# One extra matmul per step, into unused rows of the sums' PSUM tile

## The chip, the cores and the metric

The kernel runs on one core of a Trainium2 chip. The core has five engines that run at the same time, each through its own list of instructions in order: PE (TensorE, matrix multiplies; its weight loads are listed apart as PEld), ACT (ScalarE), DVE (VectorE), POOL (GpSimd) and SP (SyncE, which here only issues DMA transfers). An instruction that needs another engine's result waits for a semaphore, and everything behind it on its own engine waits too. The metric is the device time of one execution in microseconds (us); lower is better.

## The reference, cut to what matters

Four layers run one after the other on a tensor of shape 8 x 56 x 56 x 192. Layer 0 has a convolution branch and a branch with a selective scan; layers 1 and 2 are selective scans alone; layer 3 is windowed attention followed by an MLP. The part around which everything is arranged is the scan. For each image, each of three scan layers, and each of four directions k over the 56 x 56 positions:

```
def step(h, t):
    u_t, d_t, b_t, c_t = t
    h = jnp.exp(d_t[..., None] * A) * h + (d_t * u_t)[..., None] * b_t[:, :, None, :]
    return (h, jnp.einsum('bkdn,bkn->bkd', h, c_t))
scan_in = (jnp.moveaxis(xs4, -1, 0), jnp.moveaxis(delta, -1, 0), jnp.moveaxis(Bs, -1, 0), jnp.moveaxis(Cs, -1, 0))
h0 = jnp.zeros((B, K, D_INNER, D_STATE), x.dtype)
_, ys = lax.scan(step, h0, scan_in)
ys = jnp.moveaxis(ys, 0, -1) + Ds[None, :, :, None] * xs4
...
yv = _ln(yv, out_norm_g, out_norm_b) * jax.nn.silu(z)
```

There are 192 channels (d) with 16 states (n) each, so 3072 independent recurrences over 3136 positions, for 8 x 3 x 4 combinations of image, layer and direction. The sum over n with the weights c gives y, the four directions are added up, and a layer norm follows.

## The kernel before, in words

**Units and steps.** A unit (`Unit`) is one image, layer, direction and one quarter of the positions (784 of 3136); there are 8 x 3 x 4 x 4 = 384 of them. A unit is worked off in 24 steps: 2 halves of the channels (`h`, 96 each), 4 groups of 4 states (`sg`), 3 groups of 32 channels (`j`). One step holds 32 channels x 4 states = 128 recurrences on the 128 partitions. The loop in `run` goes over 9216 steps, and 8 more to drain, and writes the instruction lists of all engines in that order.

**What a step does.** `make` has ACT compute x = exp(A * delta) into one of two PSUM tiles (`ps_x`) and POOL compute db = (delta * u) * B. One step later DVE runs the recurrence as a scan (`ps_x<-ps_x,state,db` in the profile, or `hc<-ps_x,...` in every fourth step) and multiplies by C into `hc` (in every fourth step POOL multiplies instead). Two steps later ACT copies the last column to `state`, for the unit that continues there, 24 steps on. `hc` has 8 buffers.

**The sums.** Every third step, `add_up` has PE add three `hc` tiles into the PSUM tile `ps_y`: six matmuls (three channel groups j, two halves q of the columns) with the 0/1 matrix `esum` (128 x 32) as weights, `ps_y<-hc,esum` in the profile. The results of j = 0, 1, 2 go to partitions 0-31, 32-63 and 64-95. Partitions 96-127 of the two banks hold nothing. There is one such tile (`psum1`, bufs=1). After four `add_up` (12 steps) a sum is complete, and two steps later `merge` has ACT copy it to the layer's output (`act<-ps_y`). The next `add_up` starts a new tile, with two full matmuls that bring in D * u or the sum of the earlier directions (`ps_y<-act,dd`, `ps_y<-act,ident`).

**Background pieces.** All other work (the first layer's convolutions and projections of the next image, layer norms, the projection of delta, B and C, the attention and the MLP of the image before) is written as Python generators that yield between pieces. At the end of each step, `run` lets them issue pieces while a budget per engine lasts (`SPARE`, `MOST`; costs in `Engines` and `Meter`). A piece that multiplies on PE takes one of two PSUM banks (`ps_p`), and its result is fetched by ACT or DVE at the earliest one step later (`LAG = 1`). So in each engine's list, the pieces of a step follow the scan work of the step. `ahead` is the queue of pieces that prepare the next half unit (delta through softplus, du, and the transfers that spread them), `urgent` that of the layer norms and projections, `back` the rest.

**Order.** `in_order` ties each engine's instructions to the order in which they were written. A trailing part, after the last step, runs the attention of the last image alone, with more PSUM banks (`ps_t`).

Nearly all instructions carry the line of the helper that counts their cost (L109), so they are told apart by their tiles. A matmul on fp32 operands is two MATMUL records in the profile, with a weight load each.

Of the kernel before, what the change touches and what calls it, by code (L numbers as in the profile page):

```python
# [38 lines left out]
C = 192  # L39
CH = 96  # L40
# [8 lines left out]
HC = CK // 2  # L49
# [89 lines left out]
class Net:  # L139
# [146 lines left out]
    def l3_constants(self):  # L286
# [5 lines left out]
        with self.tc.tile_pool(name="setup", bufs=1) as sp:  # L292
# [12 lines left out]
            for name in ("pb", "f2b"):  # L305
# [3 lines left out]
                nc.tensor.matmul(p, self.ones, v, start=True, stop=True)  # L309
                yield LAG  # L310
                nc.vector.reduce_sum(mean[:CH, :1], p, axis=AX.X)
# [12 lines left out]
            for m in range(4):  # L324
                held = yield from self.bank()
                p = held[:, :NT]
                nc.tensor.matmul(p, w1[:, 128 * m : 128 * m + 128], tab, start=True, stop=True)
                yield LAG
                nc.scalar.activation(hid[:, m, :], p, AF.Identity, bias=b1[:, m : m + 1])
# [6 lines left out]
            for m in range(4):  # L336
                nc.tensor.matmul(p, w2[:, m, :], hid[:, m, :], start=m == 0, stop=m == 3)
            yield LAG

# [88 lines left out]
    def ln_cm(self, x, n, sq):  # L428
# [4 lines left out]
        for c in range(2):  # L433
            nc.tensor.matmul(p, self.ones, x[:, c, :], start=c == 0, stop=c == 1)
        yield LAG
        for c in range(2):
# [5 lines left out]
    def to_norm(self, x, n, sq):  # L442
# [6 lines left out]
        for c in range(2):  # L449
            nc.tensor.matmul(p, self.ones, sq[:, c, :], start=c == 0, stop=c == 1)  # L450
        yield LAG
        nc.scalar.activation(p, p, AF.Ln, bias=self.eps[:CH], scale=1.0 / C)
# [47 lines left out]
    def ssm_front(self, b):  # L500
# [3 lines left out]
        with tc.tile_pool(name="f1", bufs=1) as f1, tc.tile_pool(name="f2", bufs=2) as f2:  # L504
# [30 lines left out]
            def gate(xnt, r, e, sz):  # L535
                held = yield from self.bank()
                p = held[:CH, :T]
                nc.tensor.matmul(p, win[:, CH * e : CH * e + CH], xnt, start=True, stop=True)
                yield LAG
                if e < 2:  # L540
# [275 lines left out]
    def run(self):  # L816
        nc = self.nc
        self.B = self.a["x"].shape[0]
        units = []
        for g in range(3 * self.B):  # L820
            for o, k in enumerate((0, 1, 3, 2) if g % 2 == 0 else (2, 1, 3, 0)):
                for n, i in enumerate(range(NC) if k < 2 else range(NC - 1, -1, -1)):
                    units.append(Unit(g, k, i, n, o))
        for n, U in enumerate(units[1:]):
            units[n].next = U
        self.ranked, self.ending = None, False
        self.use_ln_exp()
        self.new_image(0)
        self.back.append(Task(self.ssm_front(0)))
        self.back.append(Task(self.conv_front(0)))  # L830
        for i in range(NC):
            self.urgent.append(Task(self.after(-1, i)))
        self.urgent.append(Task(self.columns(0)))
        self.state = self.s1.tile([128, NG], F32, name="state")
        self.B_, self.C_, self.spread = {}, {}, {}

        steps = [
            (U, h, sg, j) for U in units for h in range(2) for sg in range(NSG) for j in range(3)
        ]
        S = len(steps)  # L840
        half = NG // 2
        self.step = 0
        self.ahead.append(Task(self.prepare(units[0], 0, 0)))
        self.need(("half", 0))
        self.ahead.append(Task(self.prepare(units[0], 1, half)))
        for sg in range(NSG):
            self.load_bc(units[0], sg)
        made, weighed, copies = {}, {}, deque()
        left = dict.fromkeys(self.load, 0.0)
        for s in range(S + 8):  # L850
            self.now += 1
            self.step = s
            for e in left:
                left[e] = min(left[e] + SPARE[e], MOST[e])

            t = s + half + 1
            if t < S and t % half == 0:
                self.ahead.append(Task(self.prepare(*steps[t][:2], t)))
            if s < S and s % half == 0:
                self.need(("half", s))  # L860
                U = steps[s][0]
                if s % (16 * NG) == 0:
                    if U.l == 0:
                        self.begin_image(U.b)
                    self.dd = self.s1.tile([CH, 2, CH], F32, name="dd")
                    for c in range(2):
                        nc.scalar.activation(
                            self.dd[:, c, :], self.ident[:CH, :CH], AF.Copy,
                            scale=self.dsum[:, U.l, c : c + 1],
                        )  # L870

            t = s - 2
            if 0 <= t < S and not steps[t][0].last:
                U, h, sg, j = steps[t]
                end = CK - 1 if U.k < 2 else 0
                nc.scalar.copy(self.at_state(h, sg, j), made[t][:, end : end + 1])
            made.pop(t, None)
            if s < S:
                made[s] = self.make(*steps[s])
            t = s - 1  # L880
            if 0 <= t < S:
                U, h, sg, j = steps[t]
                x, db = made[t]
                pool = t % 4 == 3
                hc = self.s6.tile([128, CK], F32, name="hc")
                hs = hc if pool else x
                sense = slice(None) if U.k < 2 else slice(None, None, -1)
                nc.vector.tensor_tensor_scan(
                    hs[:, sense], x[:, sense], db[:, sense],
                    0.0 if U.first else self.at_state(h, sg, j), ALU.mult, ALU.add,  # L890
                )
                if not pool:
                    nc.vector.tensor_mul(hc, hs, self.C_[U, sg])
                made[t] = hs
                weighed[t] = hc
            t = s - 2
            if 0 <= t < S and t % 4 == 3:
                U, h, sg, j = steps[t]
                nc.gpsimd.tensor_mul(weighed[t], weighed[t], self.C_[U, sg])
            t = s - 4  # L900
            if 0 <= t < S and t % 3 == 2:
                U, h, sg, j = steps[t]
                self.add_up(U, h, sg, [weighed.pop(t - 2 + d) for d in range(3)])
                if sg == NSG - 1:
                    copies.append((s + 2, U, h))
            if copies and copies[0][0] <= s:
                self.merge(*copies.popleft()[1:])
            before = dict(self.load)
            while self.piece(self.ahead):
                pass  # L910
            self.spend(left, before)
            for queue in (self.urgent, self.back):
                while min(left["PE"], left["ACT"]) > 0.0 and self.piece(queue):
                    before = self.spend(left, before)

            t = s - 4
            if 0 <= t < S and t % NG >= half and t % 3 == 2:
                n = t // NG + 1
                if n < len(units):
                    self.load_bc(units[n], t % half // 3)  # L920
        while copies:
            self.merge(*copies.popleft()[1:])
        while any([self.piece(self.urgent, True), self.piece(self.back, True)]):
            self.now += 1

        self.ending = True
        self.scans.close()
        with self.tc.tile_pool(name="pst", bufs=1, space=bass.MemoryType.PSUM) as ps:
            self.banks += [ps.tile([128, 512], F32, name=f"ps_t{n}") for n in range(6)]
            self.back.append(Task(self.attention_block(self.B - 1, ENDS)))  # L930
            while self.piece(self.back, True):
                self.now += 1
        self.in_order()

    def spend(self, left, before):
        for e in left:
            left[e] -= self.load[e] - before[e]
        return dict(self.load)
# [116 lines left out]
    def add_up(self, U, h, sg, hcs):  # L1055

        nc = self.nc
        k, i = U.k, U.i
        u, y = self.bufs[U.g % 2], self.bufs[(U.g + 1) % 2]
        if sg == 0:  # L1060
            p = self.ps("y", CH, 1024).rearrange("p (q n) -> p q n", q=2)[:, :, :HC]
            for q in range(2):
                w, t = (self.dd[:, h, :], u) if U.begins else (self.ident[:CH, :CH], y)
                nc.tensor.matmul(
                    p[:, q, :], w, view(t, k, h, i * CK + q * HC, HC), start=True, stop=False
                )
            U.sums[h] = p
        p = U.sums[h]
        for q in range(2):
            for j, hc in enumerate(hcs):  # L1070
                nc.tensor.matmul(
                    p[G * j : G * j + G, q, :], self.esum, hc[:, q * HC : (q + 1) * HC],
                    start=False, stop=sg == NSG - 1,
                )
# [352 lines left out]


LAG = 1
HCS = 8  # L1430

ENDS = 5
# [130 lines left out]
```

## Time and profile before

| what | value |
|---|---|
| time, median of 3 runs | 26609.99 us (26607.5 to 26614.08) |
| the profiled execution's own time | 26624.15 us |
| its span, first to last instruction | 26622.0 us |
| mean granted TensorE clock | 0.76 of full speed |
| PE busy (matmuls) | 18403.8 us |
| DVE busy | 24146.0 us |
| POOL busy | 23082.9 us |
| ACT busy | 17059.2 us |
| 26622.0 us over 9216 steps | 2.89 us a step |

In the page of the profile, a group is one row: line, engine, operation, output<-inputs, count, then the busy time of the group, the mean of one in ns, and the idle time of the engine just before instructions of the group with what ended most of it. "PEclk" is the clock that PE was granted, in tenths. A row of the waits says who waited for whom, the sum in us, how often, and the longest. A row of the timeline is start, duration, engine, operation, tiles, shapes, how many in a row, and in brackets the idle time before it.

### The profile page before, as it was taken

The page shows a single profiled execution, that of the slowest core. Times are in us where ns is not written, and L with a number is a line of the kernel's source. Part 1 is how long each engine was busy: PE and PEld are TensorE (multiplying, and loading weights), DVE is VectorE, ACT ScalarE, POOL GpSimd, SP SyncE. Part 2 cuts the span into 40 slices and gives each one's busy share as a digit, 9 for nine tenths or more (in the row PEclk, how much of TensorE's full clock was granted, in tenths as well). Part 3 has the DMA queues.
Part 4 walks back from the last instruction along what each step waited for, and adds up shares of the span by engine and source line. Part 5 has one row for each costly group of instructions (what it writes and reads, how often), then busy time and mean ns, then how long its engine had stood idle before and what let it go on. Part 6 is the DMA issues. An engine that isn't in the chain of part 4 may idle for free. (4 is left out here: it accounts for less than half of the span.)

```text
span 26622.0 us, 260231 instructions
## 1 busy us (share of the span) xinstructions
PE 18403.8 (69%) x76788; PEld 6418.9 (24%) x76788; DVE 24146.0 (91%) x19164; ACT 17059.2 (64%) x30413; POOL 23082.9 (87%) x13255
## 2 busy tenths in 40 slices
PE   6675567776676767767767676677766777677657
PEld 2221122222222222222222222222222222222214
DVE  5999999999999999998999999999899999999994
ACT  4655566666666656666666766667666676666654
POOL 5888988988889888898888988988888888889992
PEclk7776777777777777777777777777777777777767
DMA  4565565556555566555655556555565555655551
GB/s 95 136 140 121 133 138 135 131 128 140 138 133 131 129 140 137 133 130 129 143 134 135 131 130 143 133 131 129 132 142 132 133 129 135 139 133 134 130 131 41
DMA packets 1503447, 3472.21 MB, mean 130 GB/s; under 512 B 310618, under 2 KB 503219, under 8 KB 1502020
## 3 DMA queue, kind: packets, MB, share of 16 engines
q1 hardware_dynamic: 1496452, 3455.15, 56.7%
q8 instruction: 606, 9.93, 0.1%
q0 software_dynamic: 3072, 0.31, 0.1%
q14 instruction: 821, 6.73, 0.1%
q10 hardware_dynamic: 2496, 0.09, 0.0%
HBM read 1457.23 MB, written 147.89 MB: 60 GB/s over the span
## 5 line engine op out<-in xcount | busy, mean ns | idle before, releaser
L109 POOL TENSOR_TENSOR db<-usp,bt 128x784 f32<-128x784 f32 x9216 | 16851.6, 1857 | 118.6 <-DMA usp<-du 71.4
L109 DVE TENSOR_TENSOR_SCAN ps_x<-ps_x,state,db 128x784 f32<-128x784 f32 x5184 | 9564.9, 1845 | 623.1 <-ACT state L109 266.7
L109 ACT ACTIVATE ps_x<-dsp,A 128x784 f32<-128x784 f32 x9216 | 8444.0, 917 | 2515.6 <-DVE hc L109 2290.5
L109 PE MATMUL ps_y<-hc,esum 128*32 128x392 f32 x36864 | 6882.9, 639 | 1045.1 <-POOL hc L109 696.0
L109 DVE TENSOR_TENSOR hc<-ps_x,ct 128x784 f32<-128x784 f32 x6912 | 6736.8, 975 | 654.1 <-DVE ps_x L109 11.5
L109 POOL TENSOR_TENSOR hc<-hc,ct 128x784 f32<-128x784 f32 x2304 | 4249.2, 1844 | 2448.1 <-ACT state L109 1901.2
L109 ACT COPY state<-ps_x 128x1 f32<-128x1 f32 x5184 | 823.5, 159 | 4579.7 <-DVE hc L109 4558.4
L109 DVE TENSOR_TENSOR_SCAN hc<-ps_x,state,db 128x784 f32<-128x784 f32 x1728 | 3180.1, 1840 | 230.5 <-ACT state L109 109.6
L109 DVE TENSOR_TENSOR_SCAN ps_x<-ps_x,db 128x784 f32<-128x784 f32 x1728 | 3084.8, 1785 | 275.8 <-ACT state L109 120.0
L109 PEld LDWEIGHTS ps_y<-hc,esum 128*32 128x32 f32 x36864 | 1601.2, 130 | 5928.8 <-issue 3126.8
L109 PE MATMUL ps_y<-act,ident 96*96 96x392 f32 x2304 | 1610.2, 835 | 1694.5 <-ACT act L109 1682.9
L109 PE MATMUL ps_p<-act,act 13*96 13x392 f32 (+1 forms) x3072 | 1502.9, 605 | 969.1 <-ACT s L109 294.9
L109 POOL TENSOR_TENSOR du<-delta,act 96x784 f32<-96x784 f32 x768 | 1566.5, 2040 | 66.4 <-ACT delta L109 63.9
L109 PE MATMUL ps_p<-act,wx 96*88 96x392 f32 (+1 forms) x1536 | 985.4, 778 | 627.0 <-ACT delta L109 313.4
L109 ACT ACT_TABLE_LOAD x896 | 1149.6, 1283 | 29.5 <-PE ps_p L109 13.6
L390 ACT ACT_TABLE_LOAD x897 | 1150.9, 1283 | 15.9
L109 DVE TENSOR_TENSOR_SCAN hc<-ps_x,db 128x784 f32<-128x784 f32 x576 | 1024.7, 1779 | 68.5 <-ACT state L109 35.6
L109 PEld LDWEIGHTS ps_y<-act,ident 96*96 96x96 f32 x2304 | 469.8, 226 | 2520.1 <-ACT act L109 1984.1
L109 PE MATMUL ps_p<-xip,diag 96*96 96x448 f32 x2016 | 864.0, 580 | 104.3 <-ACT delta L109 103.6
L109 ACT COPY act<-ps_y 96x784 f32<-96x784 f32 x768 | 928.0, 1208 | 8.5 <-PE ps_y L109 8.5
L109 PEld LDWEIGHTS ps_p<-act,act 13*96 13x96 f32 (+1 forms) x3072 | 471.1, 180 | 1887.5 <-issue 377.5
L109 ACT COPY state<-hc 128x1 f32<-128x1 f32 x1728 | 325.2, 188 | 866.6 <-DVE hc L109 863.9
(222 smaller groups left out, 18022.9 us busy)
## 6 DMA issues: line engine op xcount, KB each, us to landing
dsp<-delta SPq DMA_DIRECT2D x2304, 392.0 KB
usp<-du SPq DMA_DIRECT2D x2304, 392.0 KB
bt<-bcd SPq DMA_DIRECT2D x1536, 392.0 KB
ct<-bcd SPq DMA_DIRECT2D x1536, 392.0 KB
wf<-in_wf SPq DMA_DIRECT2D x128, 288.0 KB
wf<-wf2d SPq DMA_DIRECT2D x128, 288.0 KB
bcd<-bcx SPq DMA_DIRECT2D x256, 134.8 KB
szd<-sz SPq DMA_DIRECT2D x56, 336.0 KB
```

The source lines that it names most:

```text
L109: return call(out, *args, **k)
L390: self.tc.nc.scalar.preload_act_table_set(LN_EXP)
```

## The change

`add_up` now takes all 128 partitions of the `ps_y` tile and keeps rows 96-127 as `self.idle`. A new method `warm(n)` issues n matmuls into those rows: weights `esum[:96]` (96 x 32), moving operand `wout` (96 x 384), each with start and stop set, to the first bank for the first and the second bank for the second. It is called at three places of each step, with the counts in `WARM = (0, 0, 1)`: so once a step, behind the last background piece. It does nothing until the first `ps_y` tile exists. Nothing reads the result. `warm` calls TensorE directly, not through the meter, so the budget does not see it, and every other instruction of every engine stays in the same order. I call the new matmul the pad below.

```diff
@@ run
+        self.idle = None
         self.ranked, self.ending = None, False
...
             if copies and copies[0][0] <= s:
                 self.merge(*copies.popleft()[1:])
+            self.warm(WARM[0])
             before = dict(self.load)
             while self.piece(self.ahead):
                 pass
+            self.warm(WARM[1])
             self.spend(left, before)
             for queue in (self.urgent, self.back):
                 while min(left["PE"], left["ACT"]) > 0.0 and self.piece(queue):
                     before = self.spend(left, before)
+            self.warm(WARM[2])
...
+    def warm(self, n):
+
+        for q in range(n if self.idle is not None else 0):
+            self.tc.nc.tensor.matmul(
+                self.idle[:, q % 2, : 2 * C], self.esum[:CH], self.wout.rearrange("p m c -> p (m c)"),
+                start=True, stop=True,
+            )
...
@@ add_up
         if sg == 0:
-            p = self.ps("y", CH, 1024).rearrange("p (q n) -> p q n", q=2)[:, :, :HC]
+            p = self.ps("y", 128, 1024).rearrange("p (q n) -> p q n", q=2)[:, :, :HC]
+            self.idle, p = p[CH:], p[:CH]
...
 LAG = 1
+WARM = (0, 0, 1)
 HCS = 8
```

In the instruction lists of the two kernels, as built, PE has 9218 more matmuls (from the seventh pass of the loop to its last, 9224 - 6), and the other engines have the same work in the same order. Some waits differ. `merge`, which waited (where it waited for PE at all) for the last `add_up` of its sum, now waits in all 768 cases for a pad, that of the step before it. The first pad after a `merge` waits for ACT where before the first matmul of the next tile did (650 cases in both lists), and that first matmul now waits for PE's own pad.

## The prediction

> **What bounds the kernel now.** First the page: busy time by engine, and the slices with PE's granted clock.
>
> ```profile
> span 26622.0 us, 260231 instructions
> PE 18403.8 (69%) x76788; PEld 6418.9 (24%) x76788; DVE 24146.0 (91%) x19164; ACT 17059.2 (64%) x30413; POOL 23082.9 (87%) x13255
> ...
> PE   6675567776676767767767676677766777677657
> ...
> DVE  5999999999999999998999999999899999999994
> ...
> PEclk7776777777777777777777777777777777777767
> ```
>
> DVE is busy in nine tenths of nearly every slice: it sets the pace, 2.89 us a step. PE has 8218 us to spare and runs at 0.76 of its clock throughout. Then the waits, DVE's and ACT's:
>
> ```profile
> DVE ps_x L109 <- ACT state L109: 386.6, 315, 52.5
> DVE ps_x L109 <- ACT ps_x L109: 252.6, 182, 5.7
> ...
> DVE ps_p L109 <- PE ps_p L109: 65.2, 31, 39.0
> DVE act L109 <- PE ps_p L109: 60.2, 65, 6.6
> ```
> ```profile
> ACT state L109 <- DVE hc L109: 5422.3, 4498, 15.3
> ...
> ACT bcx L109 <- PE ps_p L109: 268.8, 135, 11.0
> ACT hid L109 <- PE ps_p L109: 145.6, 172, 3.5
> ACT xw L109 <- PE ps_p L109: 99.9, 38, 12.2
> ```
>
> DVE's 2476 us outside its busy time are partly short gaps between dependent instructions; counted over the trace, gaps above 150 ns make 1754 us. DVE hardly waits for PE itself, it waits for ACT when ACT is late, and ACT is late for one because it stood before a bank that PE had not filled. Counted over the 9216 steps, ACT waits 1020 us for PE, DVE 87 us. That is all that a better PE could give back. Third, the timeline of PE, where it had idled and where it had not:
>
> ```profile
> 13008.73 4.17 PE L109 MATMUL ps_p<-act,ones 96*96 96x392 f32 x6 [5.92 <-ACT act L109]
> 13012.74 1.48 PE L109 MATMUL ps_y<-act,ident 96*96 96x392 f32 x4
> 13014.15 1.52 PE L109 MATMUL ps_y<-hc,esum 128*32 128x392 f32 x12
> ```
> ```profile
> 13008.00:13012.00 4.00, 3.27 (x5) 1.52 (x6) 3.81 (x4) 1.76 (x3) 4.00 (x3) 0.50 0.12 49
> ...
> 13016.00:13020.00 4.00, 3.92 (x20) 1.38 (x18) 3.97 (x4) 2.07 (x5) 1.39 (x2) 1.00 0.51 77
> ```
>
> The second fence gives stretches with busy times by engine (PE first), then the clock, 0.50 and 1.00. After 5.92 us of idle PE runs at half clock (weight loads, and so matmul records, follow each other every 0.65 us), and some 4 us later at full clock (every 0.33 us).
>
> **What the change adds, step by step.** (1) Nothing is removed; 9218 pads are added on PE. A pad is two records of 96x384; by the nearest rows of 96x392 it costs 2 x 0.33 = 0.66 us at full clock, 1.30 us at half clock. The lower bound is nothing: twelve esum records took 1.52 us, four turns of 0.35 us and not twelve, so matmuls into different 32-row strips run beside each other, and a pad directly behind an `add_up` could too. Most pads follow a piece or another pad in the same strip, so I take 0.66 us: 6084 us of PE's 8218 us. Other engines get no instruction, SP and the DMA queues neither.
>
> (2) Where the pads run. A pad has no input of its own, so it doesn't wait until its step comes: PE runs it at once behind the matmul ahead of it in the list. In the 5.92 us of idle time above the two or three pads in front of the waiting matmul take 1.3 to 3.9 us, and the rest stays idle. So long gaps shrink but many remain. Counted over the trace, 832 gaps of PE exceed 3.4 us (5012 us together).
>
> The Trainium skill (TensorE: Matmul & The Clock Gate, Part 1 and the table under "Why this matters for your kernels") says that PE gets its full clock after about 3.4 us of activity and loses it after an idle window of that length, and advises against gaps above about 3 us. The rows above agree (0.50 after 5.92 us idle, 1.00 later). By that rule alone, with all gaps filled, this would be the best case of the first rival below; but the pads are not spread over the gaps.
>
> (3) The pieces. A matmul that ACT is seen to wait for is the end of a stretch without idle time of 11.5 us on average, at a clock of 0.70, with 1.35 pads in it (both counted over the trace, by carrying the pads' places over from the list). The pads make it 0.9 us later; the clock, if it were full all the way, 3 us earlier. I carried both down PE's list over the whole trace, idle gaps absorbing lateness, for every `ps_p` result that ACT or DVE fetches. ACT's waits on PE (1101 us in this count) become 475 us if all time lost to the half clock is won back, 776 us with three quarters of it, 1409 us with half, 2817 us with a quarter; DVE's 158 us become 72, 80, 91 and 234 us.
>
> (4) The merge. It now waits for the pad of the step before, which stands behind that step's pieces. Behind `merge` on ACT are the next state copies, the next exp (`ps_x`), which DVE's scan needs, and the pieces. One case:
>
> ```profile
> 6374.56 4.75 PE L109 MATMUL ps_p<-pada,wc 96*96 96x448 f32 x12
> ...
> 6376.30 1.62 ACT L109 COPY act<-ps_y 96x784 f32<-96x784 f32 x1
> ...
> 6378.37 0.92 ACT L109 ACTIVATE ps_x<-dsp,A 128x784 f32<-128x784 f32 x1
> ...
> 6380.90 1.85 DVE L109 TENSOR_TENSOR_SCAN ps_x<-ps_x,state,db 128x784 f32<-128x784 f32 x1
> ```
>
> The sum had been complete since 6374.6, but the pad of the step before now stands behind the twelve records that end at 6379.31. The merge would start at 6379.97 at the earliest, 3.7 us late; the exp would end near 6382 to 6383 instead of 6379.29, and the scan start 1 to 2 us late. Counted over all 768 merges: 243 start before PE has reached that pad and run it, by 421 us together at PE's present pace; by the carried lateness 187 us (all clock won back), 271, 444, and 778 us (a quarter). The merge copy now idles before only 8.5 us in all. Half of this replaces waits of pieces behind it in the same step, so I take half.
>
> (5) The pad behind a merge waits for ACT where the next tile's first matmul did; behind it stand the next `add_up`. That costs PE a pad, which is in (3), and no one else: `hc` has 8 buffers, six in use when `add_up` is issued, and in the trace no DVE multiply waited for PE.
>
> **From ACT's wait to the end.** Stretches of 12 steps in which ACT waits for PE (2.51 us on average) have 2.43 us of DVE stalls, the others 0.92 us; regressed on ACT's waits, DVE's waits and ACT's load, 0.45 of an ACT wait reaches DVE. The case in (4) loses 1 to 2 of 3.7 us, which fits. A DVE wait counts in full.
>
> **The sum.** How much of the lost clock comes back decides. I take half: the first 4 us behind a long gap stay at half clock, and the long gaps stay; what is won is the shorter gaps and a longer hold. Pieces 0.45 x (1409 - 1101) = +139 us; DVE 91 - 158 = -67 us; merges 0.45 x 444 / 2 = +100 us. Together +172 us. That prices pads at full clock; those in the slow first 4 us cost 1.30 us. With pads at 0.80 us the same count gives ACT 3024 us, DVE 315 us and merges 894 us, +1223 us. I lean a little from +172 us towards that, to +220 us: 26624 + 220 = 26844 us for the profiled execution, which is 14 us above the median, so 26,830 us.
>
> Another page speaks against the change: the Trainium skill (TensorEngine Tiling (Array Packing), Key Properties) says that changing the tiling mode drains TensorE. The pad uses 32 columns between pieces of 96. The rows show none of it: act,ident begins at 12.74 and esum behind it at 14.15, inside the 1.48 us. It gives no price, and I add none.
>
> **Rivals.** (A) Faster: the pads hold the clock. PE at full clock needs, record by record, 14,119 us of its 18,404 us, and 6084 us of pads make 20,200 us, 76% of the span, so there is room. With everything won back: 0.45 x (475 - 1101) - 86 + 0.45 x 187 / 2 = -326 us, 26,285 us. It decides from about two thirds won back; three quarters give 0.45 x (776 - 1101) - 78 + 61 = -163 us, 26,445 us. For it: the busier PE, and waits that start from runs at 0.70. Against: (2).
>
> (B) PE falls behind: a quarter won back gives 0.45 x (2817 - 1101) + 76 + 175 = +1023 us, 27,630 us. For it: in stretches of three steps the pads push PE's need at full clock over the time there is in 24% of them. Against: over 12 steps only in 6%, and being late closes gaps, which raises the clock. With no clock back ACT's waits would be 6438 us, +3.5 ms, but PE would then be busy without pause, which the rows show to end in full clock.
>
> (C) Nothing: the pads do not do what the name says, the clock stays near 0.76 where it matters, and PE's slack and ACT's (4498 waits for DVE) swallow the pads: 26,610 us.
>
> **How the numbers follow.** The forecast (0.2 to 2% slower) 0.47, A 0.26, B (over 2% slower) 0.16, C 0.11. A difference under 0.2% is about what a measurement here can't tell from none. So slower 0.63, same 0.11, faster 0.26. The range leaves out the ends of A and of B: 26,330 to 27,500 us. The likeliest case alone: 26,670 to 27,140 us.
>
> **What would show it.** Right: pads of about 0.66 us, PE busy near 23,000 us, clock 0.85 to 0.92; merges idling a few hundred us for `ps_y` pads; ACT's waits on `ps_p` the same or longer; DVE's busy time unchanged and its waits on ACT longer. Wrong: ACT's waits on PE well under 800 us (A), a clock still near 0.76, or merges that do not wait. What I trust least is the share of clock won back.

## The result and the profile after

The changed kernel takes 27376.19 us (median of 4 runs, 27365.73 to 27394.03) against 26608.75 us for the kernel before (4 runs): a ratio of 1.029, 95% interval 1.0277 to 1.0303. It is 2.9% slower; the forecast was 0.8% slower, with the range up to 27,500 us. The profiled execution's span grew from 26622.0 to 27376.8 us, by 755 us.

The page of the changed kernel: busy times, the slices of PE and DVE, and PE's granted clock in tenths.

```profile
span 27376.8 us, 296890 instructions
PE 21124.1 (77%) x95224; PEld 7082.1 (26%) x95224; DVE 24187.6 (88%) x19164; ACT 17035.9 (62%) x30413; POOL 23100.2 (84%) x13255
...
PE   6786578887787877877778877787777887788757
...
DVE  4889998998989888898998989989899898999994
...
PEclk8887778788887878878888788887877878778778
```

The busy times of DVE, ACT and POOL are what they were, to 0.2%. DVE is the pace still, and it stands still more often: its gaps above 150 ns, summed over the trace, went from 1754 to 2465 us, +711 of the 755. PE is busy 2720 us more, and its mean clock rose from 0.760 to 0.798 only. The waits of DVE and of ACT say where DVE's stalls come from (who waited for whom, us in total, times, longest).

```profile
DVE ps_x L109 <- ACT ps_x L109: 619.4, 297, 7.5
DVE ps_x L109 <- ACT state L109: 507.6, 345, 57.1
```
```profile
ACT act L109 <- PE ps_y L942: 477.7, 260, 11.0
ACT bcx L109 <- PE ps_p L109: 420.3, 156, 11.2
ACT hid L109 <- PE ps_p L109: 252.5, 249, 5.8
```

DVE's wait for exp's result (`ps_x`) rose from 252.6 to 619.4 us: ACT computes it late. ACT is late because it waits for PE. The first ACT row is new: the merge waits for the pad (L942), 477.7 us, where it had waited 8.5 us for PE before. The rows of the pieces grew too (bcx from 268.8, hid from 145.6). Over the whole trace, gaps above 150 ns, ACT's waits on `ps_p` (with `ps_t`, the banks of the trailing part) rose from 1227 to 2069 us, and DVE's own waits on PE from 320 to 404 us.

One place shows the chain whole. The timeline of the changed kernel (start, duration, engine, operation, tiles, how many; in brackets the idle time before and what ended it):

```profile
6384.68 1.90 PE L109 MATMUL ps_y<-hc,esum 128*32 128x392 f32 x9
...
6386.51 2.50 PE L109 MATMUL ps_p<-pada,wc 96*96 96x448 f32 x6
...
6388.93 0.83 PE L942 MATMUL ps_y<-wout,esum 96*32 96x384 f32 x2
...
6389.70 2.50 PE L109 MATMUL ps_p<-pada,wc 96*96 96x448 f32 x6
...
6392.12 0.83 PE L942 MATMUL ps_y<-wout,esum 96*32 96x384 f32 x2
6392.99 1.60 ACT L109 COPY act<-ps_y 96x784 f32<-96x784 f32 x1 [5.23 <-PE ps_y L942]
...
6394.64 0.92 ACT L109 ACTIVATE ps_x<-dsp,A 128x784 f32<-128x784 f32 x1
...
6395.66 1.80 DVE L109 TENSOR_TENSOR_SCAN ps_x<-ps_x,db 128x784 f32<-128x784 f32 x1 [3.41 <-ACT ps_x L109]
```

The sum that the merge copies was complete by 6386.6, with the first row. The merge stands idle 5.23 us until the pad of the step before, which is behind two groups of convolution matmuls and another pad, has run. The exp behind the merge on ACT comes late, and DVE's scan waits 3.41 us for it.

### The profile page after: what moved, and what is told of

The parts are those of the page before. It is cut to its first block, busy times and chain, and to the rows that moved or that the text cites. A ratio compares the mean times of both kernels' runs of the same rounds, so it can differ in the third digit from the quotient of the medians.

```text
span 27376.8 us, 296890 instructions
## 1 busy us (share of the span) xinstructions
PE 21124.1 (77%) x95224; PEld 7082.1 (26%) x95224; DVE 24187.6 (88%) x19164; ACT 17035.9 (62%) x30413; POOL 23100.2 (84%) x13255
## 5 line engine op out<-in xcount | busy, mean ns | idle before, releaser
L942 PE MATMUL ps_y<-wout,esum 96*32 96x384 f32 x18436 | 8344.8, 579 | 1971.4 <-ACT act L109 1874.6
L109 PE MATMUL ps_y<-hc,esum 128*32 128x392 f32 x36864 | 6354.6, 614 | 695.7 <-POOL hc L109 417.3
L942 PEld LDWEIGHTS ps_y<-wout,esum 96*32 96x32 f32 x18436 | 1812.2, 121 | 6398.0 <-issue 3883.7
L109 PEld LDWEIGHTS ps_y<-hc,esum 128*32 128x32 f32 x36864 | 1524.1, 127 | 2907.5 <-issue 1389.6
L109 PE MATMUL ps_p<-act,act 13*96 13x392 f32 (+1 forms) x3072 | 1350.8, 556 | 504.4 <-ACT s L109 133.7
L109 ACT COPY act<-ps_y 96x784 f32<-96x784 f32 x768 | 929.0, 1210 | 478.9 <-PE ps_y L942 477.7
```

The lines of the kernel that those rows point to most:

```text
L109: return call(out, *args, **k)
L942: self.tc.nc.tensor.matmul(self.idle[:, q % 2, : 2 * C], self.esum[:CH], self.wout.rearrange("p m c -> p (m c)"), start=True, stop=True,)
```

## The experiments

After the result, theory T was: the pads' PE time makes pieces late, the merge's new wait adds to it, and what the clock gives back is too little. All kernels below are edits of the changed kernel. Waits are sums over the whole trace of gaps above 150 ns; times are medians; each ratio is to runs of the kernel before that were measured together with it.

| kernel | time us | ratio to before (95%) | clock | PE busy us | ACT on ps_p | merge on pad | DVE on PE |
|---|---|---|---|---|---|---|---|
| before | 26608.75 | 1 | 0.760 | 18404 | 1227 | - | 320 |
| the change | 27376.19 | 1.0277 to 1.0303 | 0.798 | 21124 | 2069 | 478 | 404 |
| pad of 16 columns | 26977.08 | 1.0121 to 1.0151 | 0.763 | 19120 | 1599 | 294 | 351 |
| three pads behind the merge | 28127.61 | 1.0553 to 1.0585 | 0.788 | 21685 | 2753 | - | 865 |
| two pads a step | 28514.74 | 1.0698 to 1.0730 | 0.886 | 25066 | 3004 | 947 | 631 |
| pad reads a fresh hc | 27372.74 | 1.0269 to 1.0304 | 0.794 | 21920 | 2072 | 483 | 408 |
| pad over 32 rows | 29431.69 | 1.1050 to 1.1087 | 0.755 | 26534 | 3692 | 1373 | 732 |
| 16 columns, none before a merge | 26803.80 | 1.0058 to 1.0088 | 0.762 | 18940 | 1558 | - | 345 |
| pad in front of the pieces | 27484.33 | 1.0312 to 1.0342 | 0.792 | 20634 | 2279 | 71 | 676 |
| full pad, none before a merge | 27133.81 | 1.0186 to 1.0216 | 0.786 | 20479 | 1911 | - | 460 |
| pad over 128 rows | 27249.73 | 1.0230 to 1.0264 | 0.820 | 20738 | 1917 | 434 | 418 |
| whole-array pads into a pieces' bank | 26934.34 | 1.0110 to 1.0140 | 0.803 | 19869 | 1742 | - | 353 |

None is faster than the kernel before.

**The pad without its matmul time.**

```diff
-                self.idle[:, q % 2, : 2 * C], self.esum[:CH], self.wout.rearrange("p m c -> p (m c)"),
+                self.idle[:, q % 2, :16], self.esum[:CH], self.wout[:, 0, :16],
```

> The pad keeps its place, its waits and its number, but has 16 columns in place of 384, so nearly no matmul time (its result is not used either way). Theory T (the pads' PE time makes pieces late, and the merge's new wait for a pad behind the pieces adds to it; 0.46 of an ACT wait reaches DVE): the piece part goes, the merge part stays at the pace of before, 290 to 420 us of merge waits, so 26,670 to 26,800 us, ACT's waits on ps_p back near 1230 us. Rival U (the merge's wait is most of the 768 us): 27,050 us or more. Rival V (it is the number of instructions or the switch between 32 and 96 columns, not the matmul time): 27,000 to 27,380 us with ACT's waits on ps_p still near 2000 us.

1.36% slower, some 360 us: more than T gave (up to 190), less than either rival. Half of the change's loss goes with the pad's matmul time. What stays has two parts: merges still wait 294 us, as T had it, and ACT's waits on `ps_p` are 371 us above before, which T had not. PE's busy time grew by 717 us, 0.08 us for each of 9218 pads of almost no columns, so a pad isn't free when it is short.

**The same, and no pad in front of a merge.**

```diff
-            self.warm(WARM[2])
+            self.warm(0 if copies else WARM[2])
```

> Pads of 16 columns, and none in the two steps between a tile's last sum and its merge, so no merge waits for a pad. With all short pads the time was 363 us above before, with merges idle 294 us and ACT's waits on ps_p 371 us above before. If these add up as 0.46 per us, what stays is 0.46 x 371 and a little: 26,760 to 26,830 us, ps_p waits near 1550 us. If the merge's wait is the root of both (ACT late, and pieces late behind it): 26,610 to 26,680 us, ps_p waits near 1250 us.

The parts add up: 0.73% slower, inside the first range, and the `ps_p` waits are nearly unchanged (1599 to 1558 us). Against the kernel above 0.63% of the time is gone, about 170 us, with 294 us of merge waits and a sixth of the pads: 0.57 of a merge's wait, and some of that is the pads. So the merge's wait is a cost of its own and not the root of the pieces' waits.

**Full pads moved behind the merge, and full pads left out there.** Two kernels: the pads of the two steps between a tile's last sum and its merge are issued behind the merge, or not at all.

```diff
+        owed = 0
...
-            self.warm(WARM[2])
+            if copies:
+                owed += 1
+            else:
+                self.warm(1 + owed)
+                owed = 0
```

> As many pads of full size, but those of the two steps between the last sum of a tile and its merge are issued behind the merge, in the merge's step (three pads there), so the merge waits for the last sum alone. Theory T: the merge's idle time (478 us) goes, the pads' time stays: 768 - 0.46 x 478 = about +550 us, 27,100 to 27,250 us, ACT's waits on ps_p still near 2070 us or above. Rival U (the merge's wait is most of it): 26,600 to 26,800 us.

```diff
-            self.warm(WARM[2])
+            self.warm(0 if copies else WARM[2])
```

> Full pads, but none in the two steps between a tile's last sum and its merge (10 of 12 stay), so no merge waits for a pad. If moving these pads behind the merge (28,128 us) was slow because PE, just released by the merge, then has three pads in front of the next tile and the next pieces, leaving them out takes that away and the merge part too: 27,000 to 27,150 us. If the merge's wait had been holding something back that is worse when released, the time stays above 27,380 us.

Moving them was a miss: 28,128 us in place of 27,100 to 27,250, slower than the change by 750 us although no merge waits. Leaving them out gives 27,134 us, inside its range. The two differ by 994 us for the same 1536 pads (two for each of 768 merges), 0.65 us apiece: a pad's whole price at full clock. In the change the same 1536 pads stand ahead of the merge and cost 242 us (27,376 against 27,134), 0.16 us apiece, the merges' waits included. My reading: PE is blocked until the merge has run; a pad ahead of that block runs mostly in time that is idle anyway, and one behind it delays the next tile's sums and pieces by all of its time. The three pads together even use up the cover that I had named for the sums, eight `hc` buffers. DVE's wait for it, first in the kernel before, then in the one with the moved pads:

```profile
DVE hc L109 <- PE ps_y L109: 3.2, 7, 0.5
```
```profile
DVE hc L109 <- PE ps_y L109: 154.8, 172, 3.1
```

**The pad in front of the pieces.**

```diff
-WARM = (0, 0, 1)
+WARM = (1, 0, 0)
```

> The pad in front of the step's pieces, behind the sums, in place of behind the pieces. The merge then waits for a pad that has only the pieces of the steps before the last in front of it. If the two parts are separate: merges idle 200 us or less (478 in the changed kernel), ACT's waits on ps_p about as there (2069 us), time 27,200 to 27,300 us. If the place of the pad makes no difference: 27,340 to 27,420 us.

The merge's wait goes as expected, from 478 to 71 us, and yet the kernel is slower than the change by 0.4%: ACT's waits on `ps_p` are 210 us longer and DVE's on PE 272 us. A pad at the front stands before the pieces of its own step; at the back it is the next step's that it delays. The expectation took the two parts to be separate, and in this direction they are not.

**Two pads a step.**

```diff
-WARM = (0, 0, 1)
+WARM = (0, 0, 2)
```

> Two pads a step in place of one. Theory T: the lateness grows faster than the pads: 28,500 us or more, with the clock up but ACT's waits on PE (ps_p and merge) over 5000 us. Rival W (what one pad lacks is only being enough to hold the clock; with two the clock is near full and pays for them): clock over 0.92 and 27,380 us or less.

7.1% slower, as T had it; ACT's waits on PE are 3951 us, short of the 5000 I gave. The clock does rise, to 0.886, but the second pad costs 1139 us where the first cost 767.

**Why the clock came back by so little.** My reading was that pads run in a bunch and leave the long gaps open. So a pad was given an input that is made one or two steps before:

```diff
-            self.warm(WARM[2])
+            self.warm(WARM[2], weighed.get(s - 2 if s % 4 != 1 else s - 3))
...
-    def warm(self, n):
+    def warm(self, n, hc=None):
...
-                self.idle[:, q % 2, : 2 * C], self.esum[:CH], self.wout.rearrange("p m c -> p (m c)"),
+                self.idle[:, q % 2, : 2 * C], self.esum[:CH], hc[:CH, : 2 * C],
```

> The same number of pads of the same size, but the moving operand is an hc tile that DVE made one or two steps before, so a pad can't run before its step has nearly come: pads are spread over PE's idle gaps in place of running at once behind the matmul ahead. If the small win of clock (0.76 to 0.80) is due to pads bunching, the clock rises to 0.90 or more and gaps of PE above 3.4 us (604 of them after the change) nearly vanish; if the clock is then what counts, ACT's waits on ps_p fall below those of the changed kernel (2069 us) and the time is under 27,000 us. If the pads' place in PE's order counts more, the clock rises but the time is 27,380 us or more, since pieces behind a pad now wait for DVE too.

The pads did spread: PE's gaps above 3.4 us fell from 604 to 289, those above 5 us from 338 to 67 (counted over the traces; 832 and 489 before). The clock did not rise, 0.794 against 0.798, and the time is the same. The page:

```profile
PE 21919.6 (80%) x95212; PEld 7085.0 (26%) x95212; DVE 24184.2 (88%) x19164; ACT 17034.2 (62%) x30413; POOL 23098.4 (84%) x13255
...
PEclk8886678787887877888788887788877878788767
```

So bunching was not the reason. The clock in the traces changes only at steps of 3.41 us, so I cut the traces into windows of that length. In the kernel before, of the windows at half clock in which PE was busy for 95% or more, 74% were followed by full clock; in the changed kernel 63%, and those with pads in 10 to 50% of the time less often still (0.30 to 0.54). With pads in 50 to 70%, where sums run beside them in most of the time, 138 of 152 windows were followed by full clock; with pads in more of it, and hardly any sums beside them, 1 of 32. The next idea: the weights of a pad are 96 rows x 32 columns, and those of the largest matmul in any run here (the last experiment) 128 x 128; what counts may be how much of the array is at work. Two kernels change the rows that the pad sums over and leave the columns streamed at 384.

```diff
-                self.idle[:, q % 2, : 2 * C], self.esum[:CH], self.wout.rearrange("p m c -> p (m c)"),
+                self.idle[:, q % 2, : 2 * C], self.esum[:G], self.wout[:G].rearrange("p m c -> p (m c)"),
```

> The pad contracts over 32 rows in place of 96: as many columns streamed, a third of the array's rows at work. The clock came back by much less than forecast (0.76 to 0.80), and windows at half clock that hold pads rose to full clock less often (0.30 to 0.54 of them with pads in 10 to 50% of the window, 0.75 without any). If a pad wakes the clock in proportion to the array it uses, the clock falls below that of the changed kernel (0.798), to 0.77 or less, and the time rises above 27,450 us. If only the streaming time counts, clock 0.79 to 0.80 and 27,340 to 27,420 us.

```diff
+        self.wide = self.cp.tile([128, 2 * C], F32, name="wide")
+        for n in range(4):
+            self.nc.vector.tensor_copy(self.wide[:, 96 * n : 96 * n + 96], self.A[0])
...
-                self.idle[:, q % 2, : 2 * C], self.esum[:CH], self.wout.rearrange("p m c -> p (m c)"),
+                self.idle[:, q % 2, : 2 * C], self.esum, self.wide,
```

> The pad contracts over all 128 rows in place of 96, with the same 384 columns streamed (its moving operand is a constant tile of 128 partitions). If the clock goes by the share of the array at work (a sixteenth with 32 rows: clock 0.755 with PE 90% busy; three sixteenths with 96 rows: 0.798 with PE 77% busy), a quarter gives 0.81 to 0.83 and 27,100 to 27,330 us. If the share doesn't matter and the 32-row pad was slow only because it doesn't run beside the sums: clock 0.795 to 0.802, 27,340 to 27,420 us.

The page with 32 rows, and two stretches of it (length, busy time of PE, PEld, DVE, ACT and POOL with counts, clock, DMA share, GB/s):

```profile
PE 26534.4 (90%) x95224; PEld 7890.1 (27%) x95224; DVE 24240.3 (82%) x19164; ACT 17036.2 (58%) x30413; POOL 23084.5 (79%) x13255
...
PEclk7786677777777777777777777777777777777768
```
```profile
6500.00:6510.00 10.00, 10.00 (x66) 4.17 (x67) 7.75 (x8) 6.23 (x31) 10.00 (x6) 0.50 0.69 140
6510.00:6520.00 10.00, 10.00 (x28) 2.41 (x25) 9.17 (x9) 7.31 (x12) 6.49 (x5) 0.50 0.20 37
```

And the page with 128 rows:

```profile
PE 20738.3 (76%) x95224; PEld 6968.1 (26%) x95224; DVE 24185.1 (89%) x19168; ACT 17040.9 (63%) x30413; POOL 23102.4 (85%) x13255
...
PEclk8887788888888888888888888888888888888778
```

With 32 rows PE is busier than in any other kernel, and the clock is the lowest, 0.755; in the two stretches PE is busy for all of 20 us at half clock. Of the half-clock windows with PE busy for 95% or more and pads in 30% or more of the time, some 1500, only about 20 were followed by full clock. With 128 rows the clock is 0.820, PE is busy 386 us less than in the change and the time 0.4% below it, both within the range given. So the clock goes by how much of the array is at work, and the change's pad is a small part of it.

The change and the 128-row pads take the same time of PE's list (4.8 ms, each record counted to the start of the next), so it isn't the streaming time. Rows alone and rows x columns are not separated by these kernels, but the traces favour the second. Over all twelve kernels, 22,490 half-clock windows have PE busy for 95% or more. Sorted by the array's work (columns streamed x rows x columns of the weights, summed over the matmuls in the window), 12% of the lowest third, 70% of the middle and 98% of the highest were followed by full clock; sorted by rows x columns streamed 22, 61 and 98%, by columns streamed alone 26, 60 and 94%.

The 10.7% of the 32-row pad are not the clock's alone. Between two pieces at full clock it takes as long as the 96-row pad (0.76 us for the two records, start to the next matmul), but it doesn't run beside the sums: all pads take 8.5 ms of PE's list. How the 10.7% divide was not tried.

**Whole-array pads.** If share of the array times time is what wakes the clock, a short pad of 128 x 128 weights should do it cheaply. It has to go into one of the pieces' banks, when both are free, so the merge is not touched; 8388 were issued.

```diff
-            self.tc.nc.tensor.matmul(
-                self.idle[:, q % 2, : 2 * C], self.esum[:CH], self.wout.rearrange("p m c -> p (m c)"),
-                start=True, stop=True,
-            )
+            if len(self.banks) == 2:
+                self.tc.nc.tensor.matmul(
+                    self.banks[0][:, :128], self.ident, self.wide[:, :128], start=True, stop=True,
+                )
...
-WARM = (0, 0, 1)
+WARM = (0, 0, 2)
```

> Pads that use the whole array (128 rows, 128 columns, 128 streamed), two a step, about a third of the PE time of the change's pad, into a bank of the background pieces when both are free, so the merge waits for none of them. If array share times time is what wakes the clock: clock 0.80 or more, ACT's waits on ps_p at or below those of before (1227 us), 26,450 to 26,700 us. If the streaming time counts: clock 0.77 to 0.78, ps_p waits 1400 to 1800 us, 26,700 to 27,000 us.

Half of each side: the clock is 0.803, above the change's, for 1465 us of PE's busy time in place of 2720, as the first reading has it; but the time is 1.25% above before and ACT's `ps_p` waits are 1742 us, as the second has it. A wait at the banks is the likely reason, at least in part. PE's wait for the fetch of delta, in the kernel before and in this one, where the pad (L946) has it:

```profile
PE ps_p L109 <- ACT delta L109: 1916.1, 482, 15.9
```
```profile
PE ps_p L946 <- ACT delta L109: 3230.3, 733, 13.6
```

The pad has to wait until ACT has fetched what was in the bank (here delta), and the sums and pieces behind it wait with it. No kernel here raises the clock without delaying something, so what the higher clock alone is worth stays open.

## Why the prediction was right or wrong, point by point

**What bounds the kernel: right.** DVE sets the pace, PE is not on its path, and PE's lateness reaches DVE mainly through ACT. DVE's busy time did not move, its waits on ACT did.

**(1) The price of a pad: nearly right.** At full clock the median of a pad's record, start to the next record, is 0.322 us, at half clock 0.615 us, so 0.64 and 1.23 us a pad. That pads run beside the sums was named as a lower bound; it is real: counted from each record's start to the next one's, all pads took some 4850 us of PE's list, not 6084, though a quarter of them ran at half clock.

**(2) and the sum, the share of clock won back: wrong, and this is the step that failed.** I took half of the time lost to half clock to come back. On the matmuls of the pieces, which ACT waits for, about a quarter came back: their clock rose from 0.806 to 0.847, and the time that half clock cost them fell from 1839 to 1399 us, 24%. All of PE's time at half clock, idle time included, went from 12,760 to 11,080 us, 13%. The mean clock that I had named as a sign of being right, 0.85 to 0.92, was 0.798, and PE was busy 21,124 us, not near 23,000. I gave as the reason for half that long gaps stay open; the pads that were spread show that closing gaps isn't enough. What was missing is that here a matmul counted by the array it uses: with 128 rows in place of 96 the same pads gave 0.820, with 32 rows 0.755. Here the Trainium skill (TensorE: Matmul & The Clock Gate, Part 1) speaks of how busy PE is, and the runs differ from that: PE 90% busy had the lowest clock.

**(3) The pieces: mechanism right, size wrong with it.** My count gave ACT +308 us of waits on `ps_p` at half, +1716 us at a quarter won back; measured +842 us. For DVE's own waits on PE -67 and +76 us; measured +85 us. So with about a quarter won back the count asks twice too much of ACT. That it priced all pads as if none ran beside the sums goes that way; whether it is the whole reason was not tried.

**(4) The merge: right in place, near in size by luck, wrong in the halving.** 444 us of waits forecast, 477.7 us measured, but 444 was the count with half of the clock won back; for a quarter it was 778. And the case of the timeline is of the kind foreseen (5.23 us idle, scan 3.41 us late). I counted half of it on the ground that it replaces waits of pieces behind it. The kernels with 16 columns show that it does not: without merge waits, the pieces' waits stayed.

**(5) The pad behind the merge, and the cover of eight buffers: right for the change.** I wrote that no DVE multiply waited for PE before; it was 3.2 us in all, and it is 11.8 us after. Three pads there break the cover (154.8 us).

**From ACT's wait to the end: somewhat low.** I took 0.45. Fitted over the spans of nine kernels (the change and the eight experiments but for the last two in the table), 0.59 of ACT's added waits on PE, merges included, and 0.95 of DVE's give the added time: for the change 0.59 x 1320 + 0.95 x 85 = 860 us against 755 measured; for the last two, not in the fit, 756 against 626 and 335 against 273.

Put together, my own sum with the measured waits, the merge in full, is 0.45 x 842 + 85 + 0.45 x 478 = 679 us. Of the 755 us, then, the forecast's terms explain most once their sizes are right, and the size that was furthest off came from the clock.

**The rivals.** A (faster) fell with the clock. B (a quarter won back, over 2% slower) is what came, at a lower price than its 1023 us: 755. What I had against it, that PE would close its gaps and so win the clock, did not happen, with PE busy 77%; and that being busy without pause ends in full clock is wrong, as the 20 us at half clock with 32 rows show. C fell.

## What to carry to other kernels

Filler work on an engine that is off the path is paid by whoever waits for what stands behind it in that engine's list: ask for each filler which wait is ahead of it, which result is behind it, and who now waits for the filler itself. Here a filler ahead of a block cost 0.16 us and one behind it 0.65, its whole length. To raise TensorE's clock, count how much of the array the filler uses and not how long it keeps PE busy, and check the clock in the profile before counting on the gain.

## What the runs showed of the hardware that I had not expected

- The granted clock went by the array's share at work, and the window counts above bear it out. With 384 columns streamed and one pad a step: 32 rows by 32 columns, clock 0.755 with PE busy 90%; 96 by 32, 0.798 with 77%; 128 by 32, 0.820 with 76%.
- Full busy time does not mean activity. In the kernel before, among the half-clock windows with PE busy for 95% or more, some 40 were filled to 80% or more by the matmuls that open a sum, and none was followed by full clock; of about 277 filled so by the sums themselves, which run three column strips beside each other, all were. The opening matmuls read a strided view in half of the units, and a record of `ps_y<-act,ident` takes a median of 902 ns in the profile where a sum's takes 517 ns. That the strided read is the reason is argued, not shown.
- A matmul of 16 columns, weight loads included, cost PE 0.08 us of busy time, and some 7680 of them made the kernel 0.7% slower without any merge waiting for them.
